# Layer 1 of a two-layer hybrid kernel: side work in smaller pieces beside the attention units

## The chip, the cores and the metric

The kernel runs on one core of one Trainium2 chip. The metric is the device time of one launch in microseconds (us). The core has five engines that matter here. PE (TensorE) multiplies matrices into PSUM. DVE (VectorE), ACT (ScalarE) and POOL (GpSimd) work element by element. SP (SyncE) issues DMAs, one queue in program order.

## The reference, cut to what matters

The input `x` is (4, 32, 128, 128) in float32. Layer 0 is a Fourier-operator attention block; nothing of it changes here, and it ends with `x1` in device memory. Layer 1 treats each of the four batches as 4096 tokens of 128 channels. It adds additive attention over earlier tokens and then a mixture of eight experts, of which each token takes two:

```python
t = _to_tokens(x)                      # (4, 4096, 128)
t = t + _L1_attn_ref(_ln_t(t), W1, b1, w2, b2)
t = t + _L1_ffn_ref(_ln_t(t), router_w, router_b, expert_w, expert_b)

# attention: scores over all pairs i > j
t = tanh(f[:, :, None, :] + g[:, None, :, :] + b1)     # f = x W1[:h], g = x W1[h:]
e = exp(einsum('bija,a->bij', t, w2) + b2) * tril(-1)
out = (e / (e.sum(-1) + 1e-10)) @ x

# experts
p = softmax(x @ router_w + router_b); top_p, top_i = top_k(p, 2)
out = sum over the two of  top_p / sum(top_p) * (x @ expert_w[top_i] + expert_b[top_i])
```

`_ln_t` is a normalisation over the 128 channels of a token.

## The kernel before, in words

**Blocks and chunks.** One row of the picture ("image" in the code, index `k` or `t`) is a block of 128 tokens by 128 channels. A batch has 32 blocks. A chunk is eight of them (`NB`), so there are 16 chunks, four for a batch. Each half of a chunk (`h`) has 512 queries.

**Units.** A unit is one block of 128 keys against 512 queries, or two cut blocks at the diagonal. There are 528 of them, and the four chunks of a batch have 9, 25, 41 and 57. The sum of 16 hyperbolic tangents of a score is turned into products of rational terms: a numerator `n` and a denominator `d` in three groups, which PE makes by small matmuls from exponentials of queries (`qe`, `qf`) and keys (`ke`, `kf`), four at a time in four row groups of the array (L1854). ACT takes the logarithm of `d` and the exponential of its negative (L1904, L1916), DVE multiplies by `n` (L1909), POOL adds the three groups (L1912, L1913), ACT takes the exponential `e` (L1920), POOL masks the diagonal (L1925), and PE adds `e` times the normalised keys to the sum `po` (L1873). These steps are spread over five turns of the loop: turn `u` has the scores of `d` of unit `u` and of `n` of unit `u-1`, the exponential of `u-2`, and the sum of `u-4`.

**Side work.** Beside the units run three kinds of work, cut into pieces:

- For a chunk to come: a load of eight blocks into `xc` (four buffers), the normalisation into `kx` (`norm_pieces`: statistics on DVE, four small operations of `scale` on POOL, eight `apply` operations on POOL, L1519), then two transposes (L1534), keys (`as_keys`, L1569, with a multiplication on POOL and three copies by DMA) and queries (`as_queries`, L1583, with two copies).
- For a chunk that is through (`finish`): a load into `xc`; `attention`, which multiplies the sum by a centring matrix, divides, and adds it to `xc` (L1700 to L1707); a second normalisation into `x2`, again with eight `apply` on POOL; two transposes into `x2t`; the router's products and the choice of two experts (`first`, `second`, `share`, `weights`); and `experts`, one matmul of 512 columns for four experts of one block (L1760) with four DVE operations that add them by weight to `xc` (L1764); at the end the store to `out`.
- All the matmuls of these pieces share one PSUM bank, in turn (`misc`).

**What sets the order.** The loop over units is written out under a manual schedule, so every engine runs its instructions in the order of the Python code. After each unit's own work, a small planner takes pieces from queues. A piece has a kind, a cost on DVE and one on POOL in us. A unit takes at most one piece with PE work (`SOME`, `KEEPS`, `KEPT`), DVE work up to 1.8 and POOL work up to 1.7 (a first POOL piece is always taken); `gap` ends what a queue may give to this unit. Queues of chunks that are through come first, those nearly at their end last of them, then the chunk to come, unless it is short of units before it is needed (`hurry`): then it comes first. A new `finish` starts when none is under way, or one alone with at most 16 pieces left (just its experts). A chunk's load, normalisation and keys are one queue (`todo`) that starts when the chunk two before it is four units old. After the loop the rest is done one piece at a time, and two half chunks are finished.

Of the kernel before, what the change touches and what calls it, by code (L numbers as in the profile page):

```python
# [7 lines left out]
F32 = mybir.dt.float32  # L8
# [5 lines left out]
P = 128  # L14
# [10 lines left out]
NE = 8  # L25
# [1404 lines left out]
def layer1(tc, x1, w1t_in, signs, vec17, expert_w, expert_b, router_w, small_row, out):  # L1430
# [54 lines left out]
    NONE, SOME, KEEPS, KEPT, LATER = range(5)  # L1485
# [3 lines left out]
    def norm_pieces(src, dst, nb, beside=True):  # L1489
# [27 lines left out]
        def apply(k0):  # L1517
            for k in range(k0, k0 + 2):
                engine.tensor_scalar(  # L1519
                    dst[:, k], src[:, k], r[:, k : k + 1], mr[:, k : k + 1], ALU.mult, ALU.subtract  # L1520
                )
# [4 lines left out]
        for k in range(0, nb, 2):  # L1526
            after += [(NONE, 0.0, 1.6, lambda k=k: apply(k)), gap]
# [16 lines left out]
    def prepare(b, i0, own):  # L1544
# [6 lines left out]
        if c:  # L1551
            xt = work.tile([P, IC], F32, name="xt", tag="xt", bufs=1)
        else:
            xt = spare[:, NB : 2 * NB].rearrange("p k c -> p (k c)")
        if c > 1:
            xc = work.tile([P, NB, C], F32, name="xc", tag="xc", bufs=4)
            norm = normed(xc, own_kx, b, i0, True)
        else:
            norm = []

        qe, qf = (
            (work if c % 3 else first).tile([P, IC], F32, name=n, tag=n, bufs=2 if c % 3 else 1)
            for n in ("qe", "qf")
        )

        def as_keys(h):
            i = slice(i0 * P + h * 512, i0 * P + (h + 1) * 512)
            pz = misc("pz")
            nc.tensor.matmul(pz, mk, xt[:, h * 512 : (h + 1) * 512], start=True, stop=True)  # L1569
# [10 lines left out]
        def as_queries(h):  # L1580
            i = slice(h * 512, (h + 1) * 512)
            pz = misc("pz")
            nc.tensor.matmul(pz, mq, xt[:, i], start=True, stop=True)  # L1583
# [4 lines left out]
        pieces = [(SOME, 0.7, 0.0, lambda h=h: transpose_half(own_kx, xt, h)) for h in range(2)]  # L1588
# [3 lines left out]
        return (qe, qf), norm, pieces  # L1592
# [4 lines left out]
    state = {}  # L1597
    sums = {}
    live = {}

    def begin(c):
        b, i0 = chunks[c]
        if i0 == 0:

            keys = first if b % 2 == 0 else other_keys
            own = (keys.tile([P, nblk, C], F32, name=f"kx_{b}", tag="kx"),) + tuple(
                keys.tile([P, nblk * P], F32, name=f"{n}_{b}", tag=n) for n in ("ke", "kf")
            )
        else:
            own = state[c - 1][0]  # L1610
        qs, norm, pieces = prepare(b, i0, own)
        state[c] = (own, qs)
        return norm, pieces

    _, pieces = begin(0)
    kx = state[0][0][0]
# [64 lines left out]
    def finish(b, i0, nb, att, last=False):  # L1681
# [14 lines left out]
        def attention(k0):  # L1696
            pa = misc("pa")[:, : 2 * (C + 1)].rearrange("p (k c) -> p k c", c=C + 1)
            for k in range(2):
# [4 lines left out]
            rden = small.tile([P, 2, 1], F32, name="rden", tag="rden")  # L1703
            nc.vector.tensor_scalar(rden, pa[:, :, C:], 1e-10, None, ALU.add)
            nc.vector.reciprocal(rden, rden)
            for k in range(2):
# [51 lines left out]
        def experts(k, e0):  # L1758
# [305 lines left out]
```

## Time and profile before

| what | us |
|---|---|
| median of 3 runs (lowest to highest) | 2922.1 (2920.12 to 2923.42) |
| the profiled execution's own time | 2926.9 |
| its span, first to last instruction | 2925.1 |
| layer 0, and layer 1's first chunk prepared beside it | 0 to 835.6 |
| the 528 units | 835.6 to 2862.2 |
| the rest after the units | 2862.2 to 2925.1 |
| busy: PE, DVE, ACT, POOL | 2735.4, 2189.4, 2322.9, 2034.0 |

Line numbers (L1854) are those of the kernel before. Each row of a group of instructions has the line, the engine, the operation, out<-in with sizes, the count, then busy time in us and the mean of one in ns, then the idle time of the engine just before them and what ended it. In a view in order of time the first number is the start, the second the duration, both in us. Spans on POOL are rough; the spacing of starts is the surer number. A unit's time is from its first score matmul on PE to the next unit's.

### The profile page before, as it was taken

The numbers are of one execution on the slowest core, as the hardware profiler recorded it, in microseconds if no ns is written. First come the engines' busy times: TensorE is split into PE (matmuls) and PEld (weight loads), VectorE is DVE, ScalarE is ACT, GpSimd is POOL, SyncE is SP. The second block draws the span as 40 slices with busy tenths as digits, with TensorE's granted clock in tenths as the row PEclk, the third lists the DMA queues.
The fourth block names the chain that finished last, engine by engine and source line by source line (L and its number), as shares of the span: only waits on it lengthen the run. The fifth ranks groups of instructions, "written<-read, shape, count | busy, mean of one in ns | idle before, by whom it ended". The sixth has DMA issues, their size and how long they took to land.

```text
span 2925.1 us, 52645 instructions
## 1 busy us (share of the span) xinstructions
PE 2735.4 (94%) x19506; PEld 1352.7 (46%) x19506; DVE 2189.4 (75%) x4860; ACT 2322.9 (79%) x3243; POOL 2034.0 (70%) x1804
## 2 busy tenths in 40 slices
PE   8898998988878999999899999989999999999997
PEld 5565664655544444334444443434444343444443
DVE  4888788778756777666587787657778776878877
ACT  3556466455469999899899999989999998999991
POOL 1706418146139887878988887898787889798773
PEclk9999999999979999999999999999999999999998
DMA  3304205033020101011000100210000011000000
GB/s 101 123 1 112 78 15 163 13 75 101 19 77 9 25 8 33 8 33 41 19 8 17 24 15 17 49 27 14 24 17 15 19 48 26 15 19 15 15 15 15
DMA packets 151152, 107.71 MB, mean 37 GB/s; under 512 B 36302, under 2 KB 140017, under 8 KB 150897
## 3 DMA queue, kind: packets, MB, share of 16 engines
q1 hardware_dynamic: 147633, 102.26, 13.1%
q8 instruction: 154, 2.52, 0.4%
q10 hardware_dynamic: 3264, 2.10, 0.3%
q14 instruction: 101, 0.83, 0.1%
HBM read 63.86 MB, written 19.50 MB: 28 GB/s over the span
## 4 chain that ended last, share of the span: by engine, by line
PE 47%; POOL 11%; ACT 9%; issue 5%; DVE 5%; DMA 0%; POOLq 0%; SPq 0%; DVEq 0%; ACTq 0%
PE d L1854 20%; PE po L1873 12%; PE px L1760 6%; ACT r L1904 5%; PE n L1854 4%; POOL e L1913 3%; POOL e L1912 3%; ACT e L1920 2%; POOL kx L1519 1%; DVE r L1909 1%; DVE xc L1764 1%; POOL x L1519 1%; PE pl L1738 1%; POOL u L989 1%; ACT r L1916 1%
## 5 line engine op out<-in xcount | busy, mean ns | idle before, releaser
L1909 DVE TENSOR_TENSOR r<-n,r 128x1024 f32<-128x1024 f32 (+1 forms) x1056 | 962.0, 953 | 481.5 <-PE n L1854 397.9
L1912 POOL TENSOR_TENSOR e<-r 128x512 f32<-128x512 f32 x528 | 673.2, 1275 | 273.3 <-DVE r L1909 272.8
L1904 ACT ACTIVATE r<-d 128x1024 f32<-128x1024 f32 (+1 forms) x1056 | 792.9, 802 | 67.4 <-PE n L1854 59.3
L1916 ACT ACTIVATE r<-r 128x1536 f32<-128x1536 f32 x528 | 783.6, 1484 | 16.8
L1913 POOL TENSOR_TENSOR e<-e,r 128x512 f32<-128x512 f32 x528 | 671.3, 1271 | 41.4
L1854 PE MATMUL d<-qe,ke 32*128 32x512 f32 (+3 forms) x2304 | 607.5, 603 | 39.9 <-ACT r L1904 35.8
L1873 PE MATMUL po<-e,kx 128*128 128x512 f32 (+3 forms) x1152 | 594.3, 605 | 17.2 <-POOL e L1925 17.2
L1854 PE MATMUL n<-qe,ke 32*128 32x512 f32 (+3 forms) x2304 | 607.0, 602 | 0.0
L1854 PE MATMUL n<-qf,kf 32*128 32x512 f32 (+3 forms) x2304 | 553.5, 555 | 0.0
L1854 PE MATMUL d<-qf,kf 32*128 32x512 f32 (+3 forms) x2304 | 551.9, 555 | 0.0
L1764 DVE SCALAR_TENSOR_TENSOR xc<-px,wgt,xc 128x128 f32<-128x128 f32 x1024 | 358.4, 351 | 41.4 <-PE px L1760 10.6
L1920 ACT ACTIVATE e<-e 128x512 f32<-128x512 f32 x528 | 325.8, 617 | 66.0 <-POOL e L1913 65.1
L1873 PEld LDWEIGHTS po<-e,kx 128*128 128x128 f32 x1152 | 175.4, 188 | 394.6 <-issue 308.6
L1854 PEld LDWEIGHTS d<-qe,ke 32*128 32x128 f32 x2304 | 177.0, 184 | 360.2 <-ACT r L1904 340.2
L1854 PEld LDWEIGHTS d<-qf,kf 32*128 32x128 f32 x2304 | 220.7, 186 | 177.2 <-issue 164.5
L1760 PE MATMUL px<-we,x2t 128*128 128x512 f32 x512 | 265.9, 605 | 6.8 <-DVE xc L1764 5.5
L989 POOL TENSOR_TENSOR u<-xb,gb 128x858 f32<-128x858 f32 (+1 forms) x112 | 220.5, 2008 | 42.6 <-PE po L926 38.8
L1854 PEld LDWEIGHTS n<-qf,kf 32*128 32x128 f32 x2304 | 228.4, 185 | 18.9 <-issue 11.2
L1140 POOL TENSOR_TENSOR spec<-part,part 128x512 f32<-128x512 f32 x16 | 25.8, 1610 | 286.5 <-DVE gn_r_t L253 93.1
L993 DVE TENSOR_TENSOR u<-xw,gb 128x858 f32<-128x858 f32 (+1 forms) x208 | 215.4, 1100 | 6.8 <-ACT xw L980 3.2
L1854 PEld LDWEIGHTS n<-qe,ke 32*128 32x128 f32 x2304 | 177.9, 183 | 9.4 <-DVE r L1909 0.9
L926 PE MATMUL po<-u,pr 128*32 128x429 f32 (+1 forms) x1280 | 151.2, 532 | 24.9 <-POOL u L989 18.5
(425 smaller groups left out, 3378.4 us busy)
## 6 DMA issues: line engine op xcount, KB each, us to landing
xb<-xd SPq DMA_DIRECT2D x128, 214.5 KB
xc<-x SPq DMA_DIRECT2D x29, 512.0 KB
x<-x SPq DMA_DIRECT2D x16, 512.0 KB
qf<-qe SPq DMA_DIRECT2D x64, 128.0 KB
out<-xc SPq DMA_DIRECT2D x15, 512.0 KB
x<-in_x SPq DMA_DIRECT2D x14, 512.0 KB
xb<-xd SPq DMA_DIRECT2D x32, 198.0 KB
kf<-ke SPq DMA_DIRECT2D x32, 128.0 KB
```

What stands on the lines that cost most here:

```text
L989: weighed = nc.gpsimd.tensor_tensor(u, xb, gk, ALU.mult)
L993: weighed_last = nc.vector.tensor_tensor(u, xw, gk, ALU.mult)
L1760: nc.tensor.matmul(px, x2t[:, k * P : (k + 1) * P], we[:, e0 : e0 + 4], start=True, stop=True)
L1764: nc.vector.scalar_tensor_tensor(xc[:, k], px[:, e], wgt[:, k, e0 + e : e0 + e + 1], xc[:, k], ALU.mult, ALU.add)
L1854: nc.tensor.matmul(o, k, q, start=turn == 0 or g > 0, stop=turn == 1 or g > 0)
L1873: nc.tensor.matmul(sums[c, h][:, q0 : q0 + c1 - c0], kx[:, jb], e[:, c0:c1], start=jb == 0, stop=is_last and q0 > 2 * P, skip_group_check= ...
L1904: nc.scalar.activation(r[:, g], d, AF.Ln, scale=1.0 / DSCALE)
L1909: nc.vector.tensor_tensor(r[:, g], part, r[:, g], ALU.mult)
L1912: nc.gpsimd.tensor_tensor(e, r[:, 1], r[:, 2], ALU.add)
L1913: nc.gpsimd.tensor_tensor(e, e, r[:, 0], ALU.add)
L1916: nc.scalar.activation(r, r, AF.Exp, scale=-1.0)
L1920: nc.scalar.activation(e, e, AF.Exp)
```

## The change

- `experts` no longer takes four experts of one block. The products of a chunk (64, or 32) are a list of pairs of block and expert, and a call takes the next `n` of it, with one matmul for each block that they touch. It is one piece of a new kind, `EXPERTS`, which stays in its queue until the list is empty. `share_of(u)` gives `n`: products left, over units left before the last unit that they may use less the units that other PE pieces will need, rounded up, from 2 to 4.
- `attention` takes three blocks at a time where the chunk has eight (3, 3, 2), two as before in the half chunks.
- `apply` is one block (cost 0.8), each followed by a gap, and the limit of POOL work beside a unit is 0.9 where it was 1.7.
- Load and normalisation of a chunk to come are a queue of their own (`norm`), which opens as soon as the one before it is used up, from unit 4 on (from the ninth chunk on not before the keys' space of two batches earlier is free). Transposes, keys and queries (`todo`) start by the same rule as before, and take their buffers then (`place`). `hurry` is asked of both queues, with a margin of 6 and 18 units.
- `share_of`, `step` and the code after the loop follow from these.

```diff
@@ -1484,3 +1484,3 @@
 
-    NONE, SOME, KEEPS, KEPT, LATER = range(5)
+    NONE, SOME, KEEPS, KEPT, EXPERTS, LATER = range(6)
 
@@ -1516,7 +1516,6 @@
 
-        def apply(k0):
-            for k in range(k0, k0 + 2):
-                engine.tensor_scalar(
-                    dst[:, k], src[:, k], r[:, k : k + 1], mr[:, k : k + 1], ALU.mult, ALU.subtract
-                )
+        def apply(k):
+            engine.tensor_scalar(
+                dst[:, k], src[:, k], r[:, k : k + 1], mr[:, k : k + 1], ALU.mult, ALU.subtract
+            )
 
@@ -1525,4 +1524,4 @@
         after += [gap, (NONE, 0.0, 2.3, scale), gap]
-        for k in range(0, nb, 2):
-            after += [(NONE, 0.0, 1.6, lambda k=k: apply(k)), gap]
+        for k in range(nb):
+            after += [(NONE, 0.0, 0.8, lambda k=k: apply(k)), gap]
         return sums, after
@@ -1550,6 +1549,2 @@
         c = (b * nblk + i0) // NB
-        if c:
-            xt = work.tile([P, IC], F32, name="xt", tag="xt", bufs=1)
-        else:
-            xt = spare[:, NB : 2 * NB].rearrange("p k c -> p (k c)")
         if c > 1:
@@ -1559,7 +1554,14 @@
             norm = []
-
-        qe, qf = (
-            (work if c % 3 else first).tile([P, IC], F32, name=n, tag=n, bufs=2 if c % 3 else 1)
-            for n in ("qe", "qf")
-        )
+        places = {}
+
+        def place():
+
+            if c:
+                places["xt"] = work.tile([P, IC], F32, name="xt", tag="xt", bufs=1)
+            else:
+                places["xt"] = spare[:, NB : 2 * NB].rearrange("p k c -> p (k c)")
+            pool, bufs = (work, 2) if c % 3 else (first, 1)
+            for n in ("qe", "qf"):
+                places[n] = pool.tile([P, IC], F32, name=n, tag=n, bufs=bufs)
+            state[c] = own, (places["qe"], places["qf"])
 
@@ -1568,3 +1570,3 @@
             pz = misc("pz")
-            nc.tensor.matmul(pz, mk, xt[:, h * 512 : (h + 1) * 512], start=True, stop=True)
+            nc.tensor.matmul(pz, mk, places["xt"][:, h * 512 : (h + 1) * 512], start=True, stop=True)
             nc.scalar.activation(ke[:, i], pz, AF.Exp, bias=kbias)
@@ -1582,3 +1584,4 @@
             pz = misc("pz")
-            nc.tensor.matmul(pz, mq, xt[:, i], start=True, stop=True)
+            qe, qf = places["qe"], places["qf"]
+            nc.tensor.matmul(pz, mq, places["xt"][:, i], start=True, stop=True)
             nc.scalar.activation(qe[:, i], pz, AF.Exp, bias=qbias)
@@ -1587,3 +1590,3 @@
 
-        pieces = [(SOME, 0.7, 0.0, lambda h=h: transpose_half(own_kx, xt, h)) for h in range(2)]
+        pieces = [(SOME, 0.7, 0.0, lambda h=h: transpose_half(own_kx, places["xt"], h)) for h in range(2)]
         for h in range(2):
@@ -1591,3 +1594,3 @@
             pieces.append((SOME, 0.0, 0.0, lambda h=h: as_queries(h)))
-        return (qe, qf), norm, pieces
+        return norm, place, pieces
 
@@ -1597,2 +1600,3 @@
     state = {}
+    keys_of = {}
     sums = {}
@@ -1605,13 +1609,10 @@
             keys = first if b % 2 == 0 else other_keys
-            own = (keys.tile([P, nblk, C], F32, name=f"kx_{b}", tag="kx"),) + tuple(
+            keys_of[b] = (keys.tile([P, nblk, C], F32, name=f"kx_{b}", tag="kx"),) + tuple(
                 keys.tile([P, nblk * P], F32, name=f"{n}_{b}", tag=n) for n in ("ke", "kf")
             )
-        else:
-            own = state[c - 1][0]
-        qs, norm, pieces = prepare(b, i0, own)
-        state[c] = (own, qs)
-        return norm, pieces
-
-    _, pieces = begin(0)
-    kx = state[0][0][0]
+        return prepare(b, i0, keys_of[b])
+
+    _, place, pieces = begin(0)
+    place()
+    kx = keys_of[0][0]
     norms = [normed(spare[:, r], kx[:, i], 0, i.start, False) for r, i in FIRST]
@@ -1695,5 +1696,5 @@
 
-        def attention(k0):
-            pa = misc("pa")[:, : 2 * (C + 1)].rearrange("p (k c) -> p k c", c=C + 1)
-            for k in range(2):
+        def attention(k0, n):
+            pa = misc("pa")[:, : n * (C + 1)].rearrange("p (k c) -> p k c", c=C + 1)
+            for k in range(n):
                 q = (k0 + k) % QB * P
@@ -1702,6 +1703,6 @@
                 )
-            rden = small.tile([P, 2, 1], F32, name="rden", tag="rden")
+            rden = small.tile([P, 3, 1], F32, name="rden", tag="rden")[:, :n]
             nc.vector.tensor_scalar(rden, pa[:, :, C:], 1e-10, None, ALU.add)
             nc.vector.reciprocal(rden, rden)
-            for k in range(2):
+            for k in range(n):
                 nc.vector.scalar_tensor_tensor(
@@ -1757,12 +1758,26 @@
 
-        def experts(k, e0):
+        products = [(k, e) for k in range(nb) for e in range(NE)]
+
+        def experts(n):
+
+            now = products[:n]
+            del products[:n]
             px = misc("px").rearrange("p (e c) -> p e c", c=C)
-            nc.tensor.matmul(
-                px, x2t[:, k * P : (k + 1) * P], we[:, e0 : e0 + 4], start=True, stop=True
-            )
-            for e in range(4):
+            at_e = 0
+            for k in sorted({k for k, _ in now}):
+                own = [e for of, e in now if of == k]
+                m = len(own)
+                nc.tensor.matmul(
+                    px[:, at_e : at_e + m],
+                    x2t[:, k * P : (k + 1) * P],
+                    we[:, own[0] : own[0] + m],
+                    start=True,
+                    stop=True,
+                )
+                at_e += m
+            for i, (k, e) in enumerate(now):
                 nc.vector.scalar_tensor_tensor(
-                    xc[:, k], px[:, e], wgt[:, k, e0 + e : e0 + e + 1], xc[:, k], ALU.mult, ALU.add
+                    xc[:, k], px[:, i], wgt[:, k, e : e + 1], xc[:, k], ALU.mult, ALU.add
                 )
-            if k == nb - 1 and e0:
+            if not products:
                 nc.sync.dma_start(
@@ -1770,2 +1785,3 @@
                 )
+            return len(products)
 
@@ -1773,4 +1789,7 @@
         sums, after = norm_pieces(xc, x2, nb)
-        for k in range(0, nb, 2):
-            pieces += [(SOME, 1.1, 0.0, lambda k=k: attention(k)), sums[k // 2]]
+        step = 3 if nb == NB else 2
+        for k in range(0, nb, step):
+            n = min(step, nb - k)
+            pieces.append((SOME, 0.4 + 0.3 * n, 0.0, lambda k=k, n=n: attention(k, n)))
+            pieces += sums[k // 2 : (k + n) // 2]
         pieces += after
@@ -1781,7 +1800,3 @@
         pieces += [(NONE, 0.0, 0.0, share), gap, (NONE, 0.0, 1.1, weights), gap]
-        pieces += [
-            (SOME, 1.4, 0.0, lambda k=k, e=e: experts(k, e))
-            for k in range(nb)
-            for e in range(0, NE, 4)
-        ]
+        pieces.append((EXPERTS, nb * NE, 0.0, experts))
         return pieces
@@ -1887,11 +1902,30 @@
 
-    starts = [
-        (max(0, first_unit[max(0, c - 2)] + 4) if c > 1 else 0, c, first_unit[c] - 1)
-        for c in range(1, len(chunks))
-    ]
-    _, todo = begin(1)
-    starts.pop(0)
-
-
-    end, ended, ending, keeper = first_unit[1] - 1, [], [], []
+    begins = {c: first_unit[max(0, c - 2)] + 4 for c in range(2, len(chunks))}
+    opens = {c: first_unit[c - 4 - c % 4] + 4 if c >= 8 else 4 for c in begins}
+    unopened, opened = list(begins), {}
+    norm, norm_of = [], 1
+    _, place, todo = begin(1)
+    place()
+    todo_of = 1
+    ended, ending, keeper = [], [], []
+
+    def share_of(u):
+
+        queued = sum(ended, []) + todo
+        left = sum(p[1] for p in queued if p[0] == EXPERTS) + sum(NE * p[2] for p in ending)
+        others = sum(p[0] in (SOME, KEEPS) for p in queued) + NB * len(ending)
+        until = min([f + 20 * (f < first_unit[-1]) for f in first_unit if f > u] + [len(units)])
+        return min(max(-(-left // max(until - u - others, 1)), 2), 4)
+
+    def step(pieces, n):
+
+        kind, left, _, piece = pieces.pop(0)
+        if kind == EXPERTS:
+            left = piece(n)
+            if left:
+                pieces.insert(0, (kind, left, 0.0, piece))
+        else:
+            piece()
+        return kind == KEEPS and pieces[0][0] == KEEPS
+
     with tc.manual_schedule():
@@ -1936,11 +1970,21 @@
                 biases()
-            if starts and u >= starts[0][0] and not todo:
-                _, c, end = starts.pop(0)
-                todo = sum(begin(c), [])
-            if ending and (not ended or len(ended) == 1 and len(ended[0]) <= 2 * NB):
+            if unopened and not norm and u >= opens[unopened[0]]:
+                norm_of = unopened.pop(0)
+                norm, *opened[norm_of] = begin(norm_of)
+            c = todo_of + 1
+            if not todo and c in opened and (norm_of > c or not norm) and u >= begins[c]:
+                place, todo = opened.pop(c)
+                place()
+                todo_of = c
+            if ending and (not ended or len(ended) == 1 and len(ended[0]) <= 1):
                 ended.append(finish(*ending.pop(0)))
-            hurry = sum(p[0] in (SOME, LATER) for p in todo) + 6 > end - u
-            queues = sorted(ended, key=lambda p: len(p) <= 2 * NB)
-            queues.insert(0 if hurry else 2, todo)
+            hurry = [
+                q
+                for q, c in ((todo, todo_of), (norm, norm_of))
+                if q and sum(p[0] in (SOME, LATER) for p in q) + (6 if q is todo else 18) > first_unit[c] - 1 - u
+            ]
+            queues = sorted(ended, key=lambda p: len(p) <= 1)
+            queues = hurry + queues + [q for q in (todo, norm) if q not in hurry]
             pe, dve, pool = False, 0.0, 0.0
+            n = share_of(u)
             for pieces in queues:
@@ -1951,5 +1995,7 @@
                         break
-                    if kind and pe or dve + t_dve > 1.8 or pool and pool + t_pool > 1.7:
+                    if kind == EXPERTS:
+                        t_dve = 0.28 * n
+                    if kind and pe or dve + t_dve > 1.8 or pool and pool + t_pool > 0.9:
                         break
-                    if kind in (SOME, KEEPS) and keeper and keeper[0] is not pieces:
+                    if kind in (SOME, KEEPS, EXPERTS) and keeper and keeper[0] is not pieces:
                         break
@@ -1958,4 +2004,3 @@
                         keeper = [pieces] if kind == KEEPS else []
-                    pieces.pop(0)
-                    piece()
+                    step(pieces, n)
             ended = [p for p in ended if p]
@@ -1963,10 +2008,16 @@
         banks += ["n1", "d1", "n0", "d0"]
-        while ended and len(ended[-1]) > 2 * NB:
-            ended[0 if len(ended) > 1 and ended[0] else -1].pop(0)[-1]()
+        for pieces in keeper:
+            while pieces[0][0] in (KEEPS, KEPT):
+                step(pieces, 4)
+        while ended and len(ended[-1]) > 1:
+            pieces = ended[0 if len(ended) > 1 and ended[0] else -1]
+            while step(pieces, 4):
+                pass
         ended.insert(0, finish(*ending.pop(0), last=True))
         while ended:
-            for pieces in ended:
-                pieces.pop(0)[-1]()
+            for pieces in [p for p in ended if p]:
+                while step(pieces, 4):
+                    pass
                 while pieces and pieces[0][0] in (LATER, KEPT):
-                    pieces.pop(0)[-1]()
+                    step(pieces, 4)
             ended = [p for p in ended if p]
```

## The prediction

> **What bounds the kernel now.** I read the page first, for the engines over the whole span:
>
> ```profile
> span 2925.1 us, 52645 instructions
> PE 2735.4 (94%) x19506; PEld 1352.7 (46%) x19506; DVE 2189.4 (75%) x4860; ACT 2322.9 (79%) x3243; POOL 2034.0 (70%) x1804
> L1912 POOL TENSOR_TENSOR e<-r 128x512 f32<-128x512 f32 x528 | 673.2, 1275 | 273.3 <-DVE r L1909 272.8
> L1760 PE MATMUL px<-we,x2t 128*128 128x512 f32 x512 | 265.9, 605 | 6.8 <-DVE xc L1764 5.5
> ```
>
> No engine is at its end, so the mean says little. I cut the records at each unit's first score matmul (L1854), which gives 528 unit times from 835.6 to 2862.2 us. The view of windows shows what a unit is made of. Columns: stretch, length, then busy time of PE, weight loads, DVE, ACT, POOL.
>
> ```profile
> 1762.28:1793.03 30.75, 30.75 (x162) 11.20 (x161) 25.25 (x49) 28.01 (x33) 25.14 (x23) 1.00 0.06 18
> 1310.41:1327.63 17.22, 15.45 (x91) 5.88 (x91) 10.11 (x21) 17.06 (x21) 15.69 (x17) 1.00 0.00 1
> 1184.49:1216.24 31.75, 26.98 (x152) 11.39 (x153) 17.73 (x37) 25.93 (x33) 30.70 (x35) 0.95 0.00 1
> 1923.75:1960.33 36.58, 28.63 (x187) 12.86 (x187) 18.66 (x25) 28.82 (x34) 35.53 (x37) 1.00 0.06 15
> 835.59:2862.18 2026.59, 1957.31 (x11655) 858.55 (x11655) 1478.29 (x2949) 1875.37 (x2215) 1692.59 (x1590) 0.99 0.09 23
> 2862.18:2925.10 62.92, 42.69 (x113) 18.35 (x112) 48.61 (x156) 4.52 (x10) 14.55 (x26) 0.86 0.06 17
> ```
>
> Row 1: eight units with an expert piece, 3.84 us each, PE full. Row 2: five units with nothing on PE beside scores and sums, 3.44 each, ACT full (17.06 of 17.22). Rows 3 and 4: seven and eight units at 4.5 us, where POOL is full (30.70 of 31.75; 35.53 of 36.58). So there are three bounds: PE in an expert unit, ACT in a bare one, POOL in stretches.
>
> PE in time order, one expert unit:
>
> ```profile
> 1781.49 0.70 PE L1854 MATMUL d<-qe,ke 32*128 32x512 f32 x2
> ...
> 1783.42 1.12 PE L1873 MATMUL po<-e,kx 128*128 128x512 f32 x2
> 1784.39 1.02 PE L1760 MATMUL px<-we,x2t 128*128 128x512 f32 x2
> 1785.34 0.70 PE L1854 MATMUL d<-qe,ke 32*128 32x512 f32 x2
> ```
>
> The two passes of the 512-column px stand 0.43 us apart, so px is 0.86 of 3.84, and PE without it needs 2.99. Bare units take 3.43, ACT's own pace; 0.44 of PE is idle there.
>
> POOL in time order, with the group of waits of ACT in the loop:
>
> ```profile
> 1316.63 0.24 POOL L1512 TENSOR_SCALAR ln_r<-ln_mv 128x8 f32<-128x8 f32 x1
> ...
> 1319.21 1.28 POOL L1912 TENSOR_TENSOR e<-r 128x512 f32<-128x512 f32 x1
> ...
> 1327.51 1.28 POOL L1912 TENSOR_TENSOR e<-r 128x512 f32<-128x512 f32 x1
> 1328.87 1.27 POOL L1913 TENSOR_TENSOR e<-e,r 128x512 f32<-128x512 f32 x1
> 1330.12 1.57 POOL L1519 TENSOR_SCALAR kx<-xc,ln_r,ln_mr 128x128 f32<-128x128 f32 x2
> 1331.65 1.28 POOL L1912 TENSOR_TENSOR e<-r 128x512 f32<-128x512 f32 x1
> ```
>
> ```profile
> ACT e L1920 <- POOL e L1913: 60.9, 85, 1.8
> ```
>
> By spacing: two adds 2.61, two applies 1.53, so a unit with an apply piece costs POOL 4.14 against 3.43 or 3.84; a norm's scale is 2.58. ACT then waits for POOL 85 times, 60.9 us.
>
> **What the skill says.** The Trainium skill, "Perfetto Trace Analysis", GPSIMD Engine Instruction: time this engine by start-to-start spacing, not by spans. The trace agrees: an add spans 1.27 and is followed after 1.36. The same page, Optimizing Scalar/DVE Operations: profiled latency is longer than what the engine is held for, because the write's tail overlaps the next instruction. Agrees: ACT's four mean durations add to 3.71 (2x0.802+1.484+0.617) in a 3.43 unit. "TensorE: Matmul & The Clock Gate", Step-by-step: the next stationary operand loads while the present matmul runs. Agrees: px's weight load starts 2 ns after the pass before it. "PSUM — Partial Sum Buffer", The four PSUM rules: one matmul's output stays within a bank of 512 fp32; three attention products of 129 columns make 387, which fit, as two (258) did.
>
> **Floors.** A unit cannot beat the larger of ACT 3.43 and PE 2.99 plus 0.86 per 512 columns (router products: 4.67, measured). This gives 1975.8 us for the 528 units before; measured 2026.6. The excess is 50.8: 8.0 in the first nine units (start-up, bias products), 42.8 later. The latter sits where POOL is full: +4.7 in units 75 to 104, +6.8 in 141 to 165, +3.9 in 190 to 206, +10.1 in 273 to 319, +6.0 in 405 to 429, +5.9 in 9 to 33.
>
> **The change part by part.** Counts are from the built order of instructions of both programs.
>
> 1. *Experts from a list.* The same 1024 expert columns blocks and additions. Before: 229 units of the loop hold four. After: 168 hold four, 52 three, 41 two, 2 one. Above 3.43 a unit pays 0.41 with four (measured), 0.20 with three (2.99+0.64=3.63), none with two (3.42). Before 229x0.41=93.9; after 168x0.41+52x0.20=79.3: -14.6. Three or four beside a unit can straddle two images, and then px is two matmuls on the same columns: 31 such units. The extra weight load is hidden behind the running pass; were it bare, about 0.2 each (two px loads, about 0.1 of array time each by the spacing of the router's), +6 at most. DVE's additions are 0.386 apart in both; four with two statistics make 1.75+1.54+0.56=3.85 on a 3.84 unit, no loss; with an att copy besides (six units) about 0.3 each, +2.
> 2. *Attention by three.* 62 units with two images become 30 with three and 17 with two. Three cost 0.20 above the floor: +6.0. The units saved take the experts of point 1. They wait on the same bank, at the same place.
> 3. *Applies by one.* POOL's price of an apply unit falls from 4.14 to 2.61+0.76=3.37, below both floors; before, four such units added 4x0.71 of delay to 1.76 from the scale. Units 122 to 126 show what the chain bears: scale and four double applies, and yet 3.43 each; the wait begins in unit 127. By the rows that is about 3.5 us of delay (1.76+2.84, less the 0.8 POOL idled before). Bookkeeping of POOL's delay unit by unit with these spacings (masks 0.6, key multiplication 1.6) and this allowance at 3.3 gives 42 for the units after the ninth before, and 3 after; with an allowance of 2.0 it leaves 12. I take 8. Gain 42.8-8=34.8, bounds 20 and 42. POOL does the same work (1724 against 1722 by this sum): it is only moved into units with room. Also 26.3 us of PE and weight-load waits for applied images (L1534) lie in these stretches and are not counted twice.
> 4. *Norms opened early.* Loads and statistics move forward by up to 60 units: per norm one 512 KB load on SP, eight statistics and aggregates on DVE, twelve instructions on POOL. It is what lets point 3 spread. On SP the load can wait for one of four xc buffers with key and query copies queued behind. In the changed order the buffer's last reader stands in the unit of the load (41, 83, 187: POOL's last apply or the store), and the next copies are 10 or more units later: nothing, at worst a few us. Without that cover a late copy holds PE directly.
> 5. *Tail.* The loop leaves 28 expert pieces instead of 27 and three applies more; one more piece is 1.5 us of DVE, which is nearly full there (48.6 of 62.9). +1.5.
>
> Sum: -14.6+2+6.0-34.8+1.5 = -39.9, with layer 0 (to 835.6) unchanged. Against the profiled execution: span 2925.1 (its own time 2926.9) becomes 2885. The median of the runs is 2922.1, 4.8 below the profiled one; I take the change off the median: 2882.
>
> **Rivals.** *The stalls stay in part* (a chain that breaks at 1 to 2 us of POOL delay in units where ACT and PE are both tight, since expert units no longer give POOL a full 3.84): 20 of the 42.8 is gained, 2897, up to 2912. For: POOL's slack in a bare unit with one apply is only 0.06, so a scale's delay is carried for eight units. Against: the five units that bore 3.5. *Nothing happens:* the work per engine is the same and expert columns are only moved, so PE's sum stays; 2922. Against: rows 3 and 4. *Slower: POOL becomes the pace.* An apply alone might take 0.76 to 0.95 (no single apply is in the trace). Break-even with the pace is 0.82; above it delay is never made good, and each of 30 scales (1.76) and 80 masks (0.6) is paid, about 100 us less what expert units absorb, say 60 of it: 2940. It decides from an apply of about 0.9. Against: the second of a pair stands 0.76 before the next add.
>
> **How the numbers follow.** First case 0.66 (2868 to 2894), part of the stalls 0.20 (2894 to 2912), nothing 0.04, POOL the pace 0.10. The low end has no delay left and no DVE cost (-14.6+6-42.8-2, 2869), less 4 for a smoother start. Range 2865 to 2909. Within 0.2% (5.8 us, about what a measurement tells from no change) 0.03; slower 0.10; faster 0.87.
>
> **What would show it.** Right: ACT waiting for POOL falls from 60.9 to under 20; no stretch at 4.1 or more but the router's units; units with three experts at 3.63, with two at 3.43; single applies 0.76 to 0.8 before the next add; the loop at about 1986 and the tail at 64. Wrong: units of 3.5 to 3.7 with POOL full through eight applies (the pace rival), SP waiting with copies late, or px pairs apart by more than 0.43 per 512 columns.

## The result, and the profile after

The median is 2870.8 us (2870.2 to 2873.8) where the kernel before, on the same chip, has 2921.7 (2920.1 to 2923.4). The ratio is 0.9826, 95% interval 0.9814 to 0.9837, so 50.9 us are gained. The forecast was 2882, range 2865 to 2909.

The profiled execution of after takes 2870.2 us by its own time, 0.6 under its median; that of before was 5.2 over its own (2926.9 against 2921.7). So 56.5 us of difference in the spans stand for 50.9 in the medians. From the page of after, the engines and two of the groups:

```profile
span 2868.6 us, 52910 instructions
PE 2720.7 (95%) x19638; PEld 1379.6 (48%) x19638; DVE 2175.5 (76%) x4830; ACT 2315.7 (81%) x3243; POOL 2035.3 (71%) x1804
L1946 POOL TENSOR_TENSOR e<-r 128x512 f32<-128x512 f32 x528 | 673.4, 1275 | 213.0 <-DVE r L1943 211.4
L1770 PE MATMUL px<-we,x2t 128*128 128x512 f32 (+3 forms) x644 | 271.0, 515 | 5.7 <-DVE xc L1779 2.0
```

PE, DVE, ACT and POOL are as busy as before to within 15 us (POOL 2035.3 against 2034.0), on a span that is 56.5 shorter. Hardly any work went away: it was mostly waiting that did. The view of windows, with the columns used before (stretch, length, then busy time of PE, weight loads, DVE, ACT, POOL), tells where:

```profile
1161.20:1185.27 24.07, 24.07 (x141) 10.58 (x141) 19.05 (x45) 23.85 (x29) 23.35 (x23) 1.00 0.01 2
1366.21:1385.44 19.23, 19.23 (x105) 7.76 (x104) 17.23 (x44) 17.72 (x21) 18.16 (x19) 1.00 0.00 0
1103.94:1107.57 3.63, 3.63 (x21) 1.40 (x20) 3.33 (x9) 3.31 (x5) 2.34 (x3) 1.00 0.00 0
833.07:2797.56 1964.49, 1944.43 (x11785) 888.17 (x11785) 1462.87 (x2915) 1868.47 (x2215) 1691.55 (x1585) 1.00 0.10 24
2797.56:2868.57 71.01, 44.06 (x115) 19.61 (x114) 50.42 (x160) 4.53 (x10) 16.89 (x31) 0.84 0.07 19
```

Row 1 answers the stretches at 4.5 us a unit of before: seven units, each with one apply and two experts, at 3.44. POOL is still nearly full (23.35 of 24.07), but so are PE and ACT: the three now fit into one another. Row 2: five units with four experts and one apply, at 3.85. Row 3: one unit with three experts, 3.63. Rows 4 and 5 are the whole: the units fall from 2026.6 to 1964.5 (-62.1), the rest after them grows from 62.9 to 71.0 (+8.1), and the units start 2.5 earlier. That start lies at 832.6 to 837.5 in the runs below, so its 2.5 is no effect of the change.

POOL in order of time in row 1 (start, duration), and then ACT's waits within the units by group (total, times, longest):

```profile
1165.74 0.80 POOL L1518 TENSOR_SCALAR x<-xc,ln_r,ln_mr 128x128 f32<-128x128 f32 x1
1166.51 1.28 POOL L1946 TENSOR_TENSOR e<-r 128x512 f32<-128x512 f32 x1
1167.87 1.28 POOL L1947 TENSOR_TENSOR e<-e,r 128x512 f32<-128x512 f32 x1
1169.13 0.80 POOL L1518 TENSOR_SCALAR x<-xc,ln_r,ln_mr 128x128 f32<-128x128 f32 x1
1169.89 1.28 POOL L1946 TENSOR_TENSOR e<-r 128x512 f32<-128x512 f32 x1
```

```profile
ACT e L1954 <- POOL e L1947: 10.3, 18, 1.7
```

A single apply spans 0.80, and the add behind it starts 0.77 later. POOL turns round in 3.38 (1166.51 to 1169.89), under ACT's 3.43. ACT's waits for POOL fall from 85 (60.9 us) to 18 (10.3 us).

### The profile page after: what moved, and what is told of

Read it like the earlier page. It is cut to its first block, busy times and chain, and to the rows that moved or that the text cites. A ratio compares the mean times of both kernels' runs of the same rounds, so it can differ in the third digit from the quotient of the medians.

```text
span 2868.6 us, 52910 instructions
## 1 busy us (share of the span) xinstructions
PE 2720.7 (95%) x19638; PEld 1379.6 (48%) x19638; DVE 2175.5 (76%) x4830; ACT 2315.7 (81%) x3243; POOL 2035.3 (71%) x1804
## 4 chain that ended last, share of the span: by engine, by line
PE 60%; ACT 7%; DVE 5%; POOL 3%; issue 2%; DMA 0%; SPq 0%; DVEq 0%; POOLq 0%; ACTq 0%
PE d L1869 26%; PE po L1888 15%; PE px L1770 6%; PE n L1869 5%; ACT r L1938 3%; DVE r L1943 1%; ACT e L1954 1%; DVE xc L1779 1%; ACT r L1950 1%; PE pl L1739 1%; POOL e L1946 1%; PE pz L1571 1%; PE pa L1701 1%; PE pt L1533 1%; PE pz L1586 1%
## 5 line engine op out<-in xcount | busy, mean ns | idle before, releaser
L1947 POOL TENSOR_TENSOR e<-e,r 128x512 f32<-128x512 f32 x528 | 671.8, 1272 | 41.4
L1770 PE MATMUL px<-we,x2t 128*128 128x512 f32 (+3 forms) x644 | 271.0, 515 | 5.7 <-DVE xc L1779 2.0
L1770 PEld LDWEIGHTS px<-we,x2t 128*128 128x128 f32 x644 | 119.3, 193 | 140.4 <-issue 116.8
```

Source lines behind the costliest of these rows:

```text
L1770: nc.tensor.matmul(px[:, at_e : at_e + m], x2t[:, k * P : (k + 1) * P], we[:, own[0] : own[0] + m], start=True, stop=True,)
L1947: nc.gpsimd.tensor_tensor(e, e, r[:, 0], ALU.add)
```

## The experiments

All times are medians, with the 95% interval of the ratio to the kernel before on the same chip (its medians there are 2921.7 to 2922.9). "Units" and "rest" are the two parts of the profiled execution; "floor" is the sum of the prediction's prices (the larger of ACT 3.43 and PE 2.99 plus 0.86 for 512 columns; 4.67 with the router's products) over the units in that kernel's own order, and "excess" is what the units take over it.

| kernel | median us | ratio | units | floor | rest |
|---|---|---|---|---|---|
| before | 2921.7 | 1 | 2026.6 | 1975.8 | 62.9 |
| before with single applies | 2895.7 | 0.9908 (0.9893 to 0.9923) | 1972.9 | 1972.9 | 87.5 |
| after, always four experts, attention by two | 2874.7 | 0.9837 (0.9822 to 0.9851) | 1978.7 | 1979.5 | 58.9 |
| after, always four experts | 2873.4 | 0.9837 (0.9822 to 0.9852) | 1980.9 | 1986.1 | 56.2 |
| after | 2870.8 | 0.9826 (0.9814 to 0.9837) | 1964.5 | 1967.1 | 71.0 |
| after, run again | 2871.0 | 0.9817 (0.9803 to 0.9832) | 1964.6 | 1967.1 | 71.0 |
| after, applies by two | 2908.7 | 0.9951 (0.9934 to 0.9968) | 2009.6 | 1964.9 | 63.2 |
| after, each apply beside a unit twice | 3024.2 | 1.0342 (1.0321 to 1.0362) | 2110.1 | 1967.1 | 77.5 |
| after, norms not opened early | 2887.3 | 0.9879 (0.9865 to 0.9894) | 1963.9 | 1967.7 | 87.1 |
| after, attention by two | 2865.5 | 0.9799 (0.9784 to 0.9813) | 1958.7 | 1961.0 | 70.9 |
| after, last chunk's pieces sooner | 2867.5 | 0.9808 (0.9792 to 0.9824) | 1964.3 | 1967.1 | 65.5 |
| after, both of these | 2860.0 | 0.9785 (0.9767 to 0.9803) | 1959.0 | 1961.0 | 65.5 |

One price in this floor is too high, and in every row alike. The sum counts the four transposes of a half chunk (`pt`) as 512 columns, and so their unit at 3.84. Two such units of the kernel before, with nothing that holds them up, show what they take. The first two lines are in time order, the third is the window of both units:

```profile
1276.97 0.60 PE L1534 MATMUL pt<-ident,kx 128*128 128x128 f32 x4
1277.50 0.70 PE L1854 MATMUL d<-qe,ke 32*128 32x512 f32 x2
1274.08:1280.97 6.89, 6.89 (x46) 3.25 (x45) 5.53 (x10) 6.56 (x8) 5.10 (x4) 1.00 0.27 76
```

The next unit starts 0.53 after the first transpose, and the two units take 6.89, or 3.44 each. Every kernel here has 58 to 61 units with transposes; in after their median is 3.44. At a price of 3.43 each, the floors of before and of after would be some 24 us lower, about 1951 and 1943. The differences between the rows are not touched by this. But "at the floor" below means at this sum, and not that no time is lost.

### Single applies alone, on the kernel before

```diff
-        def apply(k0):
-            for k in range(k0, k0 + 2):
+        def apply(k):
...
-        for k in range(0, nb, 2):
-            after += [(NONE, 0.0, 1.6, lambda k=k: apply(k)), gap]
+        for k in range(nb):
+            after += [(NONE, 0.0, 0.8, lambda k=k: apply(k)), gap]
...
-            hurry = sum(p[0] in (SOME, LATER) for p in todo) + 6 > end - u
+            hurry = sum(p[0] in (SOME, LATER) for p in todo) + 18 > end - u
...
-                    if kind and pe or dve + t_dve > 1.8 or pool and pool + t_pool > 1.7:
+                    if kind and pe or dve + t_dve > 1.8 or pool and pool + t_pool > 0.9:
...
-            for pieces in ended:
+            for pieces in [p for p in ended if p]:
```

> The kernel before with one edit: the norm's applies one block at a time, POOL work beside a unit limited to 0.9 (the chunk to come is put in a hurry 12 units earlier, so that its keys are still in time). Experts by four, attention by two, no early opening. Theory P (POOL's double applies made the stalls): the 528 units fall from 2026.6 us to about 1973 (the floor of its own order of pieces, 1972.9 by the prices of the prediction), ACT waits for POOL under 20 us; the rest after the units grows by about 15 us, as 34 expert pieces instead of 27 and more of another chunk are left; in all about 2890. Rival S (what counts is how the expert products are spread): the units stay within 10 us of 2026 and the time is 2920 or more.

Measured: 2895.7 us, 26.5 less than before on the same chip. ACT's waits within the units, and the windows of units and rest:

```profile
ACT e L1919 <- POOL e L1912: 8.0, 10, 1.7
```

```profile
834.17:2807.12 1972.95, 1939.28 (x11633) 860.70 (x11633) 1464.43 (x2905) 1867.16 (x2215) 1690.71 (x1584) 1.00 0.09 23
2807.12:2894.64 87.52, 50.94 (x135) 23.02 (x134) 61.36 (x200) 4.52 (x10) 17.59 (x32) 0.81 0.09 24
```

The units fall by 53.6 and stand at their floor. Of this, 2.9 is a lower floor and 3.6 lies in the first nine units (excess 4.4 instead of 8.0; 4.2 to 4.4 in every other run, whatever its order); 47.1 is left for the stalls. So this edit by itself brings the gain in the units, and takes ACT's waits from 60.9 to 8.0, with experts still by four and attention still by two. But the rest grows by 24.6, where about 15 had been expected: DVE has 61.36 us to do there instead of 48.61, because work that no longer found a unit was left to the end. Nearly half of the gain in the units is given back.

### Always four experts, with attention by two and by three

```diff
-        return min(max(-(-left // max(until - u - others, 1)), 2), 4)
+        return 4
...
-        step = 3 if nb == NB else 2
+        step = 2
```

The first kernel has both hunks, the second only the first.

> The changed kernel with experts always by four and attention by two: applies by one and norms opened early alone. Theory P: units at their floor, 1979 us, the rest after them about 60 (22 expert pieces), in all about 2873, so nearly the whole gain without any spreading. Rival S: most of the gain is lost, 2905 or more.

> The changed kernel with experts always by four (attention by three, applies by one, norms early). Theory P: units about 1984 us against 1964.5 with two to four (floors 1986.1 and 1967.1), the rest about 60 instead of 71 as 21 pieces are left instead of 28; in all about 2877. Rival S: 2900 or more.

Measured: 2874.7 and 2873.4 us. ACT's waits for POOL within the units, first with attention by two, then by three:

```profile
ACT e L1954 <- POOL e L1947: 5.7, 9, 1.7
```

```profile
ACT e L1954 <- POOL e L1947: 5.2, 9, 1.7
```

Both kernels stand at or under their floors, like after, so the spread of experts has no part in removing stalls. What it does is seen in the windows of the second kernel beside those of after:

```profile
834.67:2815.60 1980.93, 1952.69 (x11678) 867.19 (x11678) 1482.51 (x2955) 1870.85 (x2218) 1697.06 (x1597) 1.00 0.10 24
2815.60:2871.84 56.24, 33.25 (x89) 14.83 (x88) 38.12 (x120) 3.82 (x7) 11.69 (x19) 0.82 0.07 19
```

Spread, the experts make the units 16.4 us shorter (1980.9 to 1964.5) and the rest 14.8 us longer (56.2 to 71.0), where DVE's work grows from 38.12 to 50.42. The list has fewer products beside a unit, so more of them are left when the units end: 28 px matmuls in after, 21 in this kernel. In all the spread is worth some 2.6 us of median; the two medians are from different sets of runs, and this difference is near what the measurement can tell.

### Applies by two again, in the kernel after

```diff
-        def apply(k):
+        def apply(k0):
+            for k in range(k0, k0 + 2):
...
-        for k in range(nb):
-            after += [(NONE, 0.0, 0.8, lambda k=k: apply(k)), gap]
+        for k in range(0, nb, 2):
+            after += [(NONE, 0.0, 1.6, lambda k=k: apply(k)), gap]
...
-                    if kind and pe or dve + t_dve > 1.8 or pool and pool + t_pool > 0.9:
+                    if kind and pe or dve + t_dve > 1.8 or pool and pool + t_pool > 1.7:
```

> The changed kernel with applies two at a time and the POOL limit at 1.7 again (experts two to four, attention by three, norms early). Theory P: POOL's stalls come back, about 37 us above the floor of 1964.9, units about 2000, in all about 2898, ACT waits for POOL 40 us or more. Rival S: units at 1965 or below, in all about 2865.

Measured: 2908.7 us. ACT's waits within the units, and POOL in order of time through a row of double applies:

```profile
ACT e L1955 <- POOL e L1948: 56.6, 84, 1.8
```

```profile
1181.47 1.28 POOL L1947 TENSOR_TENSOR e<-r 128x512 f32<-128x512 f32 x1
1182.82 1.28 POOL L1948 TENSOR_TENSOR e<-e,r 128x512 f32<-128x512 f32 x1
1184.09 1.57 POOL L1519 TENSOR_SCALAR x<-xc,ln_r,ln_mr 128x128 f32<-128x128 f32 x2
1185.63 1.27 POOL L1947 TENSOR_TENSOR e<-r 128x512 f32<-128x512 f32 x1
```

The turn is 4.16 (1181.47 to 1185.63) in units that ACT could do in 3.43. The first four units with a pair still take 3.43 to 3.49, and the two behind them 4.15 and 4.39: the delay builds up over some units before it shows. Before had 85 waits of this kind, and here are 84 of them, and the excess over the floor with them: 44.7 (about 37 had been expected), against -2.6 in after, so 47.3 more. The rest is 7.9 shorter, so the total rises by 37.9.

### Each apply beside a unit done twice

```diff
-            engine.tensor_scalar(
-                dst[:, k], src[:, k], r[:, k : k + 1], mr[:, k : k + 1], ALU.mult, ALU.subtract
-            )
+            for _ in range(2 if beside else 1):
+                engine.tensor_scalar(
+                    dst[:, k], src[:, k], r[:, k : k + 1], mr[:, k : k + 1], ALU.mult, ALU.subtract
+                )
```

> The changed kernel with each POOL apply issued twice (the second writes the same values): POOL again pays 4.14 us in an apply unit, and nothing else moves. Theory P: about 110 us above the floor (240 apply units, their delay only made good in the units between), units 2060 to 2085, in all 2970 to 2990. Rival (POOL has room and the stalls came from the neighbourhood of other pieces): units below 2000, in all under 2910.

Measured: 3024.2 us. ACT's waits within the units:

```profile
ACT e L1955 <- POOL e L1948: 166.8, 200, 2.4
```

The order is that of after; only POOL's load grows, by 232 applies and 178.7 us within the units. The excess becomes 143.0, where about 110 was expected. A good part of what lies between is probably in the edit itself. Five units in a row with two experts and a double apply take 4.25 to 4.27 each, where the prices of the prediction give 4.14. POOL in order of time in the second of them:

```profile
1209.44 1.27 POOL L1947 TENSOR_TENSOR e<-r 128x512 f32<-128x512 f32 x1
1210.79 1.27 POOL L1948 TENSOR_TENSOR e<-e,r 128x512 f32<-128x512 f32 x1
1212.04 1.69 POOL L1519 TENSOR_SCALAR x<-xc,ln_r,ln_mr 128x128 f32<-128x128 f32 x2
1213.69 1.27 POOL L1947 TENSOR_TENSOR e<-r 128x512 f32<-128x512 f32 x1
```

The turn of POOL is itself 4.25 (1209.44 to 1213.69). The second apply writes the block that the first has just written, and it starts 0.89 after it (median of 232 pairs), where in a pair on two blocks, in the kernel before, it starts 0.78 after it (117 pairs). By these numbers the 232 pairs hold some 28 us more of POOL than pairs on two blocks would; this is an estimate. So the run says that POOL's load sets the pace of such units, and its size can't be set beside that of the kernel before without this difference.

### Norms opened late

```diff
-    opens = {c: first_unit[c - 4 - c % 4] + 4 if c >= 8 else 4 for c in begins}
+    opens = begins
```

> The changed kernel with the norms of chunks to come opened only when their keys may start (the rule of the kernel before). Theory P: applies by one alone remove the stalls, so the units stay at their floor of 1967.7 us; what early opening buys is room, and without it more is left for the end: 32 expert pieces and eight transposes instead of four, the rest 80 to 88 instead of 71, in all about 2884. Rival (applies by one need the early opening to find units with room): units 1980 or more.

Measured: 2887.3 us. The units are 1963.9, no longer than in after, and ACT waits 6.2 us for POOL in them. So the early opening is not what lets single applies fit. It is worth 16.1 us in the rest (87.1 against 71.0), where DVE has 58.74 us of work instead of 50.42, and 32 px matmuls are left instead of 28.

### Attention by two images

```diff
-        step = 3 if nb == NB else 2
+        step = 2
```

> The changed kernel with attention two blocks at a time. By the prices of the prediction attention by three loses: 30 units at 3.63 instead of 3.43, and the units that it saves are left bare (83 bare units against 68), so the floor is 1961.0 against 1967.1. That theory: units 1958, in all about 2865. Rival (the freed units take experts, so three is a gain): 2872 or more.

Measured: 2865.5 us (2864.1 to 2866.3), against 2871.0 (2869.9 to 2871.7) for after on the same chip. The units are 5.8 shorter, the floor 6.1, the rest is as it was. Three images cost what their columns cost; the fifteen units that they save bring nothing back.

### The end: the last chunk's own pieces sooner

The last chunk is finished as two half chunks. After the units, the code first takes pieces until the first half has no more than one left, those of the chunk before it ahead of its own, and only then lets the pieces of the last half in turn with what remains. In the kernel before, the limit was `2 * NB` pieces; the first half had 16 left there, so nothing was drained, and the experts of the chunk before went in turn with the rest. With the experts in a single piece, the limit became one, and they are used up first. The edit leaves them:

```diff
-        while ended and len(ended[-1]) > 1:
+        while ended and len(ended[-1]) > 2 * NB:
```

Here the first half has fewer than `2 * NB` pieces left, so the drain does not run.

> The changed kernel with one number of the code after the loop put back: the last half chunk is begun as soon as the one before it has 16 pieces left or fewer, instead of only its experts. Theory T (the rest grew from 62.9 to 71.0 us because the last half chunk's norm, router and weights now run with no expert products beside them; DVE is idle for 8.2 us there in four waits): rest about 63, in all 2863. Rival (it grew because more work was left, 28 expert pieces for 27 and three applies): no more than 2 us less, 2869 or more.

Measured: 2867.5 us (2865.4 to 2869.3); rest 65.5 instead of 71.0. The median falls by 3.5 only: two of the four executions are at 2865 to 2866, two at 2869, and the profiled one is the fastest of them. DVE's waits in the last part of the rest, first of after and then of this kernel:

```profile
DVE xc L1779 <- POOL wgt L1757: 2.9, 2, 1.4
DVE x2t L1534 <- PE pt L1533: 2.9, 1, 2.9
DVE top L1725 <- PE pl L1739: 2.0, 1, 2.0
```

```profile
DVE top L1725 <- PE pl L1739: 2.0, 1, 2.0
DVE xc L1779 <- POOL wgt L1757: 1.4, 1, 1.4
```

With expert additions still in hand, DVE has something to do while the last norm is applied and transposed: the wait for the transposes goes, and one of two for the weights. The other two stay; they come last in the chain of the last half chunk, where probably nothing is left to fill them. So the reason is right in kind, and smaller than the four waits together: 4.4 of their 7.8 us go, and the rest is 5.5 shorter, where about 8 had been expected.

### Both of these edits

> Two edits together: attention by two images, and the last chunk's own pieces brought in before the drain of the previous one ends. A (the two gains are of different stretches and add): units as with attention by two alone, 1958.7 give or take 1; the rest as with the tail edit alone, 65.4 give or take 2; in all 2871.0 - 5.5 - 3.5 to 5.5, so 2860 to 2862, ratio 0.978 to 0.979. B (the attention edit shifts which pieces are left for the rest, as the expert pieces left behind were moved by other edits, and takes back what the tail edit gives): units 1958.7 but rest 69 or more, 2864 to 2867.

```profile
837.55:2796.59 1959.04, 1937.53 (x11790) 888.55 (x11791) 1467.11 (x2945) 1866.66 (x2215) 1693.44 (x1585) 1.00 0.10 24
2796.59:2862.06 65.47, 41.58 (x115) 17.53 (x114) 49.74 (x160) 4.53 (x10) 16.94 (x31) 0.86 0.06 16
```

Measured: 2860.0 us (2858.9 to 2863.8), ratio 0.9785 (0.9767 to 0.9803). The two gains are of different stretches and add: units 5.5 shorter than after's, rest 5.5 shorter. By its median this kernel is faster than either.

### Smaller shares of experts, further apart

Two kernels, both with the two edits above, let a chunk's experts reach 40 and 50 units into the next chunk instead of 20, the first also with at most three experts beside a unit before the fifteenth chunk (the second one's edit is shown):

```diff
-        until = min([f + 20 * (f < first_unit[-1]) for f in first_unit if f > u] + [len(units)])
+        until = min([f + 50 * (f < first_unit[-1]) for f in first_unit if f > u] + [len(units)])
```

> A version meant to beat both: the changed kernel with attention by two, the last half chunk begun earlier (as in the run on the rest), experts spread over 40 instead of 20 units into the next chunk, and never more than three beside a unit before the last two chunks. Floor of its order 1933.4, 36 expert pieces and eight attention blocks left. If the floors hold: units 1932, rest 80 to 85, in all about 2850. Rival (the slip of ACT and PE against each other already gives what the floors promise, so smaller pieces gain nothing more): units 1950 or more, in all 2866 or more.

> The same with up to four experts beside a unit and the spread over 50 units: floor 1947.0, 30 expert pieces left. If the floors hold: units 1945, rest about 68, in all about 2850. Rival as for the run before: units 1955 or more, in all 2862 or more.

Spread so far, a `finish` can be late for the next, and what still waits when the units end is left out: of the 17 `finish` of layer 1 (load, attention, norm, router, experts, store) the first kernel leaves out two and the second one. So neither computes the whole output, and their times, 2855.0 and 2852.6 us, can't be set beside the others. Their units, 1936.6 and 1951.8, stand 3.2 and 4.8 over the floors of their own orders (1933.4 and 1947.0), 6 to 7 us further up than those of after do. The first lies nearer to what was expected if the floors hold (1932, against 1950 or more), the second between the two (1945, against 1955 or more). Whether a wider spread would gain with all of the work done stays open.

## Why the prediction was right, and which of its terms were not

The side, the mechanism and the range were right: POOL's double applies held ACT, and single ones fit beside a unit. The time came 11 us lower than the forecast. By its own steps:

1. *Experts from a list* (-14.6, +2). The prices held: 3.43 with two, 3.63 with three, 3.84 with four (medians of after). A px split over two images costs 0.01 more (3.85), so its cover held. The att copies beside four experts and two statistics cost some 0.2 in five of six units, 1.1 in all where 2 was allowed. By the runs the list takes 16.4 out of the units against always four. What the step did not say is that almost all of this comes back in the rest (14.8), which the kernel with always four experts shows: its order leaves 21 px matmuls for the end, and that of after 28.
2. *Attention by three* (+6.0). Measured by undoing it: 5.8 in the units, 5.5 of median.
3. *Applies by one* (-34.8, bounds 20 and 42). This is the term that was mis-sized. Alone on the kernel before it gave 47.1 of excess after the first nine units; undone in the kernel after, it cost 47.3. Outside the first nine units the excess goes from 42.8 to -7.0: 49.8 are gained, more than the 42.8 that the step took for all there was. That ceiling was too low, because the floor from which it was read prices the units with transposes at 3.84 where they take 3.44. With 3.43 for the 58 of them outside the first nine, some 67 us of excess stood there before, and some 17 remain. So it isn't shown that no delay is left over. ACT still waits 10.3 us for POOL in the units of after; what else the 17 hold was not traced. The first nine units, taken as unchanged at 8.0, have 4.4. Together with the 2 us of point 1, a part of this same excess, that is 15.0 + 3.6 + 2 = 20.6, all of the difference between -41.4 worked out for the units and -62.1 measured. The first nine units have the same pieces in the kernel before and in that with single applies alone, and take 3.6 less there, so that difference is of the execution and no effect of the change.
4. *Norms opened early* (nothing, "it is what lets point 3 spread"). The first half held: no late copy shows. The second is false. With the norms opened late the units are as short (1963.9), probably because the margin of 18 units for the norm's queue leaves room enough. What the step brings is 16.1 us in the rest, which the prediction counted nowhere.
5. *Tail* (+1.5). It grew by 8.1. DVE's work there rose by 1.8 (48.61 to 50.42), as the step said; the other 6.3 are DVE idle. The step counted a piece and overlooked the order after the loop: with experts as one piece, the drain takes the filler away before the last half chunk needs it. The edit at the end returns 5.5 of it.

Together: the units gained 20.7 more than worked out, the rest lost 6.6 more, and the start gave 2.5, which makes the spans' 56.5 out of 39.9. The 3.6 of the first nine units and the 2.5 of the start belong to the profiled execution of before, which ran 5.2 over its median. What is left, 15.0 + 2 - 6.6 = 10.4, is about the 11 us by which the medians missed the forecast. The two errors have opposite signs, and that the range held is in part luck: with a tail as forecast the time would have been near 2864, just under the range's low end of 2865.

Two sums of the prediction do not come out. The delay borne in units 122 to 126 is 3.8 by its own terms (1.76+2.84-0.8), not 3.5. And the low end, with no delay left and no DVE cost, is -14.6+6.0-42.8+1.5 = -49.9, or 2872, less 4 for the start 2868; the text takes off 2 more for a cost that its other terms do not hold, and leaves out the tail. The forecast rests on neither, and the measured time lies above both low ends.

The rivals. *Stalls stay in part* (a gain of only 20 of the 42.8) is out: the gain is 49.8 here and 47 where only the applies differ, and wherever each apply is single and done once, the units come to within 5 us of the floor or below it. *Nothing* is out with it. *POOL becomes the pace* needed an apply of 0.9; it is 0.77 by spacing, under the break-even of 0.82. The kernel with each apply twice shows what that rival would have looked like on a larger scale: 200 waits of ACT and a time 3.4% above before. Of the signs named in advance, the waits held (10.3, under 20), as did the prices of units with two and three experts and the 0.77 behind a single apply. The loop came out lower than said, 1964 instead of 1986, and the rest higher, 71 instead of 64. No long stretch stands at 4.1 or more, though besides the router's 26 other units behind the ninth take that long, most of them singly.

## What to carry to other kernels

Cut side work so that one piece fits the slack of each engine in its unit; applies in pairs cost some 47 us more here than the same applies in separate units. A side piece that stays under the other bound is free and one that exceeds it pays by the column: 256 columns beside a unit cost nothing, 384 cost 0.20, so larger pieces that save units need not gain. Take the price of each kind of piece from units of its own in the trace: one wrong price, that of the transposes, made the gain to be had look 24 us smaller than it was. Where a planner moves pieces, look at the end as well: smaller shares leave more for after the loop, and code there that counts pieces changes its meaning when a piece becomes a list.

## What the runs showed that I had not expected

- The sum over units of the larger of two engines' prices is not a strict floor, even apart from the transposes. Bare units beside PE-bound ones take 3.09 (20 with at most statistics and their aggregates, median), less than ACT's 3.43; over the 80 bare units of after behind the ninth this makes some 11 us. The reading that fits is that ACT, which has waited for PE in the unit before, is only a part of a unit late or early against it and makes that up; it was not tested apart.
- A delay on POOL is borne for some four units before ACT waits (3.43 to 3.49 with a turn of 4.16).
- Two applies on the same block are dearer than two on different blocks: the second starts 0.89 after the first instead of 0.78.
- Four transposes of 128 columns cost PE about half of what 512 columns of a product do: they start 0.11 apart (median over the units of after), which is 0.44 for the four, where px takes 0.86.
